# Mamba recurrence in pairs of tiles: 1024-column products and scans, states in SBUF over their inputs

## The chip, the core and the metric

The kernel runs on one core of a Trainium2 chip, as one launch. The metric is the device time of that launch in microseconds, lower being better. The core's engines work side by side and meet at semaphores: PE (TensorE, matrix products into PSUM), DVE (VectorE, elementwise work and scans), ACT (ScalarE, activation functions), POOL (GpSimd, elementwise work and indirect transfers) and SP (SyncE, which here issues most transfers). SBUF is the working memory of 128 partitions, PSUM the smaller memory that PE writes. All values here are fp32.

## The reference, cut to what matters

The program is a two-layer hybrid network over 32 sequences of 256 tokens and 128 features. The change concerns its first block alone, a bidirectional Mamba: 256 inner channels, 16 states per channel, forward and backward.

```python
def step(h, inp):
    u_t, d_t, B_t, C_t = inp
    dA = jnp.exp(d_t[..., None] * A)
    h = dA * h + (d_t * u_t)[..., None] * B_t[:, None, :]
    y = jnp.sum(h * C_t[:, None, :], axis=-1)
    return (h, y)
h0 = jnp.zeros((Bb, D_INNER, D_STATE), x.dtype)
_, ys = lax.scan(step, h0, xs)
y = jnp.transpose(ys, (1, 0, 2)) + xc * Dskip
y = y * jax.nn.silu(z)
return y @ out_w.T
...
y_f = _mamba(xn, ...)
y_b = jnp.flip(_mamba(jnp.flip(xn, 1), ...), 1)
y = jnp.concatenate([y_f, y_b], axis=-1) @ proj_w.T + proj_b
return x + y
```

After it come expert blocks, a tanh recurrence and two attention blocks with routed experts. They are the same before and after the change.

## The kernel before

The residual stays in SBUF as 16 tiles `xs[c]` of 128 features x 512 tokens (two sequences). The Mamba stage runs 32 units, `unit(k)`: chunk `k // 2`, forward for even k and backward for odd k. A unit is a Python generator; `pipeline(unit, 16, 2 * NCH)` starts a new one every 16 yields, so that the preparation of one unit (norm, convolution, projections, softplus) is traced beside the recurrence of the one before. The framework orders the instructions of each engine from this trace when it schedules them, by readiness and priority; so the order on an engine can differ from the order in the code. `behind_scans()` holds a DVE instruction behind the last scan traced.

**Preparation.** L425 to L530 make the activated input `act`, the step sizes `delta`, `du = delta * act` and the `gate`. Softplus is done with ACT functions and then three DVE instructions over 128x1024 values, L508 to L510, all of whose tensors lie in SBUF; the product L511 is POOL's. `delta` and `du` go to DRAM and come back (L545) as `widedelta` and `widedu`, with 4 states' copies on neighbouring partitions; B and C come back as `bcB` and `bcC` (L534). All these transfers are issued on SP.

**Recurrence.** A unit has two halves h of the channels, and in each four groups g of four tiles k. A tile is 128 partitions (32 channels x 4 states) x 512 columns. For each tile:

- L602, ACT: `dA = exp(A * delta)` into one of three PSUM banks `dAs`, taken in turn. Columns 0 and 256 stay zero from the memset at L407, so that the scan starts anew at each sequence.
- L606, POOL: `dBu = du * B`, 128x512, in SBUF.
- L615, DVE: the scan `h = dA * h + dBu`. Tiles 0 to 2 write their states to PSUM (`h2`), tile 3 to SBUF (`hs`). The backward direction reads and writes in reverse.
- The product with C: one DVE instruction for tiles 0 and 1 together (L617, 128x1024), one for tile 2 (L625, 128x512); tile 3 goes to POOL (L563)[...]. Of L617's and L625's operands, the states lie in PSUM and `bcC` in SBUF.

The weighted states of a group are summed over the 4 states of each channel by PE into the bank `yps` (L568), together with the skip product (L566). `summed` for one group is called after the second tile of the next. After four groups, DVE multiplies `yps` by the gate (L584); the backward unit also projects and adds to the residual (L637, L638).

[...]: three `dAs`, two `m`, two `hs`, one `yps`.

Of the kernel before, what the change touches and what calls it, by code (L numbers as in the profile page):

```python
# [13 lines left out]
F32 = mybir.dt.float32  # L14
# [3 lines left out]
AF = mybir.ActivationFunctionType  # L18
ALU = mybir.AluOpType
# [3 lines left out]
P = 128  # L23
B, L = 32, 256
NT = B * L
CH = 512
# [247 lines left out]
def hybrid_kernel(ctx: ExitStack, tc, x_d, out_d, d, packs):  # L274
    nc = tc.nc
# [14 lines left out]
    def K(name):  # L290
        return cst.view(cst_t, name) if name in cst.at else cst1.view(late_t["cst1"], name)
# [10 lines left out]
    def two(ap):  # L302
        return ap.rearrange("p (b t) -> p b t", b=2)
# [48 lines left out]
    with ExitStack() as ph:  # L352
# [7 lines left out]
        wconv, wout, A, skip = {}, {}, {}, {}  # L360
        with tc.tile_pool(name="mtap", bufs=1) as tp, tc.tile_pool(name="mprep", bufs=2, space=PSUM) as pp:
            tap_t = tp.tile([P, tap.n], F32, name="tap_t")
            nc.scalar.dma_start(tap_t, d["tap"].partition_broadcast(P))
            for k, s in enumerate("fb"):

                wconv[s] = wp.tile([P, DCONV, DI], F32, name="wconv" + s)
                at, _, w = tap.at[s]
# [20 lines left out]
        p2 = ph.enter_context(tc.tile_pool(name="m2", bufs=2))  # L388
        ps = ph.enter_context(tc.tile_pool(name="mps", bufs=2, space=PSUM))
# [7 lines left out]
        outs, turn, scan = {}, [0], [None]  # L397

        def behind_scans():

            return tc.issue_after(scan[0].ins) if scan[0] else nullcontext()

        dAs = [ps.tile([P, CH], F32, name=f"dA{k}", bufs=1) for k in range(3)]
        for t in dAs:
            nc.vector.memset(two(t)[:, :, 0:1], 0.0)  # L407

        def rows_of(ap, at, dims, n_rows):

            return bass.AP(ap.tensor, ap.offset + at * CH, [[a * CH, n] for a, n in dims] + [[1, n_rows * CH]])

        def unit(k):
            c, s = k // 2, "fb"[k % 2]
# [5 lines left out]
            def both(tag, bufs):  # L420
                return p2.tile([P, 2, CH], F32, tag=tag, name=tag, bufs=bufs)
# [45 lines left out]
            for h in range(2):  # L467
                for j in range(DCONV):
                    at = j if s == "f" else 2 * PAD - j
# [4 lines left out]
                        start=(j == 0),  # L474
                        stop=False,
# [5 lines left out]
            act = both("act", 2)  # L481
# [38 lines left out]
            for h in range(2):  # L520
# [4 lines left out]
                    start=True,  # L525
                    stop=True,
                )
            yield
            gate = both("gate", 2)
            nc.scalar.activation(gate, m, AF.Silu)  # L530
            bc = {}
# [9 lines left out]
            def load(h):  # L541
                out = []
                for n in ("delta", "du"):
                    t = p2.tile([P, 4, CH], F32, tag="wide" + n, name="wide" + n)
                    nc.sync.dma_start(  # L545
                        t.rearrange("p k t -> p (k t)"), rows_of(wide_d[n], h * P, ((4, 32), (0, 4)), 4)
                    )
                    out.append(t)
                return out
# [5 lines left out]


            sums, ended = None, None
            yps = None

            def summed(h, g, prods, hs):  # L560
                nonlocal yps, ended
                pr = p2.tile([P, CH], F32, tag="prod", name="pr", bufs=4)
                nc.gpsimd.tensor_mul(pr, hs, bc["C"][:, g, :])  # L563
                if g == 0:
                    yps = ps.tile([P, CH], F32, tag="y", name="yps", bufs=1)
                    nc.tensor.matmul(yps, skip[s][:, h, :], act[:, h, :], start=True, stop=False, skip_group_check=True)  # L566
                for k, pr in enumerate([*prods, pr]):
                    nc.tensor.matmul(  # L568
                        yps[32 * k : 32 * k + 32, :],
                        K("states"),  # L570
                        pr,
                        start=False,
                        stop=(g == 3),
                        skip_group_check=True,
                        tile_position=(0, 32 * k),
                    )
                if g == 3:
                    ended = h

            def gated():  # L580
                nonlocal ended
                yg = p2.tile([P, CH], F32, tag=f"yg{s}{ended}", name="yg", bufs=1)
                with behind_scans():
                    nc.vector.tensor_mul(yg, yps, gate[:, ended, :])  # L584
                outs[s, ended] = yg
                ended = None

            for h in range(2):
                dw, duw = wide[h]
                for g in range(4):  # L590
                    if (h, g) == (0, 1):
                        wide.append(load(1))

                    h2 = ps.tile([P, 2, CH], F32, tag="hs", name="h2", bufs=1)
                    pr2 = p2.tile([P, 2, CH], F32, tag="prod2", name="pr2", bufs=2)
                    prods = [pr2[:, 0, :], pr2[:, 1, :]]
                    for k in range(4):
                        dA = dAs[turn[0] % 3]
                        turn[0] += 1
                        at = 16 * h + 4 * g + k  # L600
                        steps = dw[:, k, :] if s == "f" else dw[:, k, ::-1]
                        nc.scalar.activation(  # L602
                            two(dA)[:, :, 1:L], two(steps)[:, :, 1:L], AF.Exp, scale=A[s][:, at : at + 1]
                        )
                        dBu = p2.tile([P, CH], F32, tag="dBu", name="dBu", bufs=4)
                        nc.gpsimd.tensor_mul(dBu, duw[:, k, :], bc["B"][:, g, :])  # L606
                        if k == 3:
                            hs = p2.tile([P, CH], F32, tag="hs", name="hs")
                        elif k == 2:
                            h2 = ps.tile([P, 2, CH], F32, tag="hs", name="h2", bufs=1)  # L610
                            hs = h2[:, 0, :]
                        else:
                            hs = h2[:, k, :]
                        views = (hs, dA, dBu) if s == "f" else (hs[:, ::-1], dA, dBu[:, ::-1])
                        scan[0] = nc.vector.tensor_tensor_scan(*views, 0.0, ALU.mult, ALU.add)  # L615
                        if k == 1:
                            nc.vector.tensor_mul(pr2, h2, bc["C"][:, g, :].unsqueeze(1).to_broadcast([P, 2, CH]))  # L617
                            yield
                            if ended is not None:
                                gated()  # L620
                            if sums:
                                summed(*sums)
                        elif k == 2:
                            pr = p2.tile([P, CH], F32, tag="prod", name="pr", bufs=4)
                            nc.vector.tensor_mul(pr, hs, bc["C"][:, g, :])  # L625
                            prods.append(pr)
                    sums = (h, g, prods, hs)
                    yield
            yield
            summed(*sums)  # L630
            yield
            gated()
            yield
            if s == "b":
# [4 lines left out]
                yield  # L639

        pipeline(unit, 16, 2 * NCH)

    late = ctx.enter_context(tc.tile_pool(name="late", bufs=1))
# [1066 lines left out]
```

## Time and profile before

| | us |
|---|---|
| median of 3 runs | 6272.99 |
| the three runs | 6271.46 to 6285.75 |
| profiled execution, its own time | 6280.36 |
| profiled execution, its span | 6278.6 |

| engine, whole span | busy us | share |
|---|---|---|
| PE | 5317.6 | 85% |
| DVE | 4184.9 | 67% |
| POOL | 3335.2 | 53% |
| ACT | 2664.6 | 42% |

The shares are means over stages with different limits. The Mamba stage takes about the first third: between 60 and 2100 us DVE is busy for 1866.63 us, POOL for 1770.79, PE for 1447.34 and ACT for 1170.29. Lines of the profile name the source line, the engine, the operation, the tile written and those read, shapes and count, and then busy time and mean duration in ns of one instruction, followed by the engine's idle time ahead of them and what ended it. A line of the timeline gives the start and the duration in us.

### The profile page before, as it was taken

To read this page: it belongs to the slowest core of one execution; us is meant where nothing else is said; L and a number is where in the kernel's file an instruction comes from. 1 tells how busy PE (TensorE), PEld (TensorE's weight loads), DVE (VectorE), ACT (ScalarE), POOL (GpSimd) and SP (SyncE) were. 2 spreads that over 40 slices of the span, in tenths; PEclk is the share of its full clock that TensorE was granted. 3 is DMA by queue.
4 is the path that set the end of the run, shared out by engine and by line. 5 is a ranking of instruction groups with operands and counts; after the bars stand their busy time and mean duration, and the time that the engine had idled before them with its cause. 6 is when DMAs were issued, how large, how long until landed. Compare 5 with 4: busy or idle time off the path is not lost. (4 is left out here: it accounts for less than half of the span.)

```text
span 6278.6 us, 73286 instructions
## 1 busy us (share of the span) xinstructions
PE 5317.6 (85%) x25538; PEld 2731.4 (44%) x25538; DVE 4184.9 (67%) x7070; ACT 2664.6 (42%) x4376; POOL 3335.2 (53%) x3074
## 2 busy tenths in 40 slices
PE   6777777777776799999989889897998999998897
PEld 2111111111111366865534444445884444444786
DVE  5999999999999664044645555554665666664565
ACT  4565555556565355334524434432221333333221
POOL 5888888888888565034634444443332333333332
PEclk8887888888888899588989999998998999997998
DMA  3232233322332660000000000003550000000555
GB/s 153 115 122 115 108 129 121 116 108 112 119 122 114 235 257 1 1 1 1 1 1 8 9 10 8 8 11 104 188 188 22 18 18 18 18 11 11 188 187 187
DMA packets 190417, 512.08 MB, mean 82 GB/s; under 512 B 22176, under 2 KB 75168, under 8 KB 164960
## 3 DMA queue, kind: packets, MB, share of 16 engines
q1 hardware_dynamic: 172192, 468.00, 20.7%
q0 software_dynamic: 17280, 35.69, 1.7%
q8 instruction: 202, 3.31, 0.2%
q10 hardware_dynamic: 576, 3.71, 0.2%
q14 instruction: 167, 1.37, 0.1%
HBM read 359.93 MB, written 147.38 MB: 81 GB/s over the span
## 5 line engine op out<-in xcount | busy, mean ns | idle before, releaser
L606 POOL TENSOR_TENSOR dBu<-widedu,bcB 128x512 f32<-128x512 f32 x1024 | 1334.0, 1324 | 250.7 <-DVE h L615 132.8
L615 DVE TENSOR_TENSOR_SCAN h<-dA,dBu 128x512 f32<-128x512 f32 x768 | 941.3, 1226 | 108.7 <-ACT dA L602 37.8
L568 PE MATMUL yps<-pr,cst_t 128*32 128x512 f32 x2048 | 702.5, 719 | 300.0 <-POOL pr L563 129.4
L930 POOL TENSOR_SCALAR_AFFINE_SELECT e<-e 128x2048 f32<-128x2048 f32 (+1 forms) x256 | 343.1, 1352 | 600.7 <-ACT e L1041 388.5
L1406 POOL DMA_INDIRECT rows_out<-y,goes x284 | 271.8, 957 | 558.5 <-DVE y L1404 451.5
L602 ACT ACTIVATE dA<-widedelta,Af 128x510 f32<-128x510 f32 x512 | 351.3, 689 | 398.4 <-DVE h L615 311.0
L994 DVE TENSOR_REDUCE nm<-st 128x2 f32<-128x512 f32 x512 | 324.3, 684 | 267.6 <-PE st L990 266.7
L602 ACT ACTIVATE dA<-widedelta,Ab 128x510 f32<-128x510 f32 x512 | 346.9, 687 | 354.5 <-DVE h L615 237.1
L568 PEld LDWEIGHTS yps<-pr,cst_t 128*32 128x32 f32 x2048 | 98.8, 120 | 870.2 <-POOL pr L563 308.1
L1181 ACT ACTIVATE s<-s 128x512 f32<-128x512 f32 x284 | 179.0, 630 | 575.9 <-DVE s L1180 329.2
L314 POOL TENSOR_TENSOR rstd<-var,cst_t 128x4 f32<-128x4 f32 x128 | 130.0, 1016 | 514.0 <-DVE var L312 512.1
L775 POOL TENSOR_TENSOR comb<-comb,ye 128x512 f32<-128x512 f32 x224 | 284.7, 1275 | 181.2 <-DVE ye L774 74.8
L1054 ACT ACTIVATE e<-st 128x512 f32<-128x512 f32 x512 | 271.6, 599 | 178.0 <-PE st L1050 146.0
L563 POOL TENSOR_TENSOR pr<-hs,bcC 128x512 f32<-128x512 f32 x256 | 339.8, 1328 | 13.3 <-DVE hs L615 13.0
L615 DVE TENSOR_TENSOR_SCAN hs<-dA,dBu 128x512 f32<-128x512 f32 x256 | 308.9, 1207 | 16.5 <-ACT dA L602 16.5
L1295 POOL DMA_INDIRECT rows_in<-xt,slot x256 | 254.0, 992 | 119.5 <-issue 99.1
L617 DVE TENSOR_TENSOR pr<-h,bcC 128x1024 f32<-128x1024 f32 x256 | 309.9, 1210 | 7.8
L1182 DVE TENSOR_TENSOR hh<-s,u_ps 128x512 f32<-128x512 f32 x284 | 195.3, 688 | 169.8 <-ACT s L1181 165.5
L1387 PE MATMUL g_ps<-xb,gu 128*128 128x256 f32 x1136 | 302.1, 389 | 3.6 <-ACT xb L1370 2.3
L1396 PE MATMUL yps<-dn,hh 128*128 128x128 f32 x2272 | 290.6, 276 | 5.3 <-DVE hh L1182 5.3
L1387 PE MATMUL u_ps<-xb,gu 128*128 128x256 f32 x1136 | 293.4, 381 | 0.0
L1396 PEld LDWEIGHTS yps<-dn,hh 128*128 128x128 f32 x2272 | 282.4, 192 | 14.0 <-DVE hh L1182 6.8
(348 smaller groups left out, 11021.0 us busy)
## 6 DMA issues: line engine op xcount, KB each, us to landing
gu<-in_gu SPq DMA_DIRECT2D x142, 512.0 KB, 3.7
rows_in<-zero SPq DMA_DIRECT2D x60, 1170.0 KB, 18.7
widedelta<-delta_d SPq DMA_DIRECT2D x64, 1024.0 KB, 6.8
widedu<-du_d SPq DMA_DIRECT2D x64, 1024.0 KB, 5.1
dn<-in_dn SPq DMA_DIRECT2D x142, 256.0 KB, 3.9
bcB<-xdbl_d SPq DMA_DIRECT2D x32, 1024.0 KB, 5.3
bcC<-xdbl_d SPq DMA_DIRECT2D x32, 1024.0 KB, 7.2
xr<-rows_in SPq DMA_DIRECT2D x142, 130.0 KB, 3.9
```

Source lines behind the costliest of these rows:

```text
L563: nc.gpsimd.tensor_mul(pr, hs, bc["C"][:, g, :])
L568: nc.tensor.matmul(yps[32 * k : 32 * k + 32, :], K("states"), pr, start=False, stop=(g == 3), skip_group_check=True, tile_position=(0, 32 ...
L602: nc.scalar.activation(two(dA)[:, :, 1:L], two(steps)[:, :, 1:L], AF.Exp, scale=A[s][:, at : at + 1])
L606: nc.gpsimd.tensor_mul(dBu, duw[:, k, :], bc["B"][:, g, :])
L615: scan[0] = nc.vector.tensor_tensor_scan(*views, 0.0, ALU.mult, ALU.add)
L617: nc.vector.tensor_mul(pr2, h2, bc["C"][:, g, :].unsqueeze(1).to_broadcast([P, 2, CH]))
L775: nc.gpsimd.tensor_add(comb, comb, ye)
L930: nc.gpsimd.affine_select(e, e, [[0, n], [sign, P]], ALU.is_gt, 0.0, base=base, channel_multiplier=-sign)
L994: nc.vector.tensor_reduce(n1[:, x, 2 * r : 2 * r + 2], o.rearrange("p (j k) -> p j k", j=2), AX.X, ALU.max, negate=True,)
L1387: nc.tensor.matmul(o[:, j, :], gu[:, at : at + P], xb, start=True, stop=True)
L1396: nc.tensor.matmul(yps[:, t, :], hh[:, k, t * P : (t + 1) * P], dn[:, k, :], start=(k == 0), stop=(k == FF // P - 1),)
L1406: i = nc.gpsimd.indirect_dma_start(rows_out[:, :], bass.IndirectOffsetOnAxis(ap=goes[:, t : t + 1], axis=0), y[:, t, :], None)
```

## The change

The four tiles of a group are handled as two pairs of 128x1024.

- `dAs` become two tiles of two PSUM banks each, taken in turn by pairs. ACT still writes 128x512 at a time; backward, the two halves are swapped, and ACT reads the steps in reverse.
- One POOL product over 1024 columns writes `du * B` of a pair into an SBUF tile `hs` (six buffers). One DVE scan over 1024 columns runs in place, its states replacing their inputs. The zeros in `dA` separate the tiles of a pair as they do the sequences.
- The product with C is in place, too, over 1024 columns (`weigh`): on DVE for the first pair; for the second pair on POOL, except in the fourth group of a half, where it is DVE's. It is called for the second pair in `summed`, after the first pair of the next group.
- `yps` has two banks, one for each half; the states' two PSUM banks are gone.

The matmuls, the transfers and all other stages are unchanged.

```diff
-        dAs = [ps.tile([P, CH], F32, name=f"dA{k}", bufs=1) for k in range(3)]
+        dAs = [ps.tile([P, 2, CH], F32, name=f"dA{k}", bufs=1) for k in range(2)]
         for t in dAs:
-            nc.vector.memset(two(t)[:, :, 0:1], 0.0)
+            nc.vector.memset(t.rearrange("p k (b t) -> p (k b) t", b=2)[:, :, 0:1], 0.0)
...
-            def summed(h, g, prods, hs):
-                nonlocal yps, ended
-                pr = p2.tile([P, CH], F32, tag="prod", name="pr", bufs=4)
-                nc.gpsimd.tensor_mul(pr, hs, bc["C"][:, g, :])
+            yps = {}
+
+            def weigh(engine, hs, g):
+                engine.tensor_mul(hs, hs, bc["C"][:, g, :].unsqueeze(1).to_broadcast([P, 2, CH]))
+
+            def summed(h, g, pairs):
+                nonlocal ended
+                weigh(nc.vector if g == 3 else nc.gpsimd, pairs[1], g)
                 if g == 0:
-                    yps = ps.tile([P, CH], F32, tag="y", name="yps", bufs=1)
-                    nc.tensor.matmul(yps, skip[s][:, h, :], act[:, h, :], start=True, stop=False, skip_group_check=True)
-                for k, pr in enumerate([*prods, pr]):
+                    yps[h] = ps.tile([P, CH], F32, tag="y", name="yps")
                     nc.tensor.matmul(
-                        yps[32 * k : 32 * k + 32, :],
+                        yps[h], skip[s][:, h, :], act[:, h, :], start=True, stop=False, skip_group_check=True
+                    )
+                for k in range(4):
+                    nc.tensor.matmul(
+                        yps[h][32 * k : 32 * k + 32, :],
                         K("states"),
-                        pr,
+                        pairs[k // 2][:, k % 2, :],
...
-                    nc.vector.tensor_mul(yg, yps, gate[:, ended, :])
+                    nc.vector.tensor_mul(yg, yps[ended], gate[:, ended, :])
...
-                    h2 = ps.tile([P, 2, CH], F32, tag="hs", name="h2", bufs=1)
-                    pr2 = p2.tile([P, 2, CH], F32, tag="prod2", name="pr2", bufs=2)
-                    prods = [pr2[:, 0, :], pr2[:, 1, :]]
-                    for k in range(4):
-                        dA = dAs[turn[0] % 3]
+                    pairs = []
+                    for half in range(2):
+                        dA = dAs[turn[0] % 2]
                         turn[0] += 1
-                        at = 16 * h + 4 * g + k
-                        steps = dw[:, k, :] if s == "f" else dw[:, k, ::-1]
-                        nc.scalar.activation(
-                            two(dA)[:, :, 1:L], two(steps)[:, :, 1:L], AF.Exp, scale=A[s][:, at : at + 1]
+                        for k in range(2):
+                            at = 16 * h + 4 * g + 2 * half + k
+                            steps = dw[:, 2 * half + k, :]
+
+                            a = dA[:, k if s == "f" else 1 - k, :]
+                            steps = steps if s == "f" else steps[:, ::-1]
+                            nc.scalar.activation(
+                                two(a)[:, :, 1:L], two(steps)[:, :, 1:L], AF.Exp, scale=A[s][:, at : at + 1]
+                            )
+
+                        hs = p2.tile([P, 2, CH], F32, tag="hs", name="hs", bufs=6)
+                        nc.gpsimd.tensor_mul(
+                            hs, duw[:, 2 * half : 2 * half + 2, :], bc["B"][:, g, :].unsqueeze(1).to_broadcast([P, 2, CH])
                         )
-                        dBu = p2.tile([P, CH], F32, tag="dBu", name="dBu", bufs=4)
-                        nc.gpsimd.tensor_mul(dBu, duw[:, k, :], bc["B"][:, g, :])
-                        if k == 3:
-                            hs = p2.tile([P, CH], F32, tag="hs", name="hs")
-                        elif k == 2:
-                            h2 = ps.tile([P, 2, CH], F32, tag="hs", name="h2", bufs=1)
-                            hs = h2[:, 0, :]
-                        else:
-                            hs = h2[:, k, :]
-                        views = (hs, dA, dBu) if s == "f" else (hs[:, ::-1], dA, dBu[:, ::-1])
-                        scan[0] = nc.vector.tensor_tensor_scan(*views, 0.0, ALU.mult, ALU.add)
-                        if k == 1:
-                            nc.vector.tensor_mul(pr2, h2, bc["C"][:, g, :].unsqueeze(1).to_broadcast([P, 2, CH]))
+                        flat = hs.rearrange("p k t -> p (k t)")
+                        flat = flat if s == "f" else flat[:, ::-1]
+                        scan[0] = nc.vector.tensor_tensor_scan(
+                            flat, dA.rearrange("p k t -> p (k t)"), flat, 0.0, ALU.mult, ALU.add
+                        )
+                        pairs.append(hs)
+                        if half == 0:
+                            weigh(nc.vector, hs, g)
                             yield
...
-                        elif k == 2:
-                            pr = p2.tile([P, CH], F32, tag="prod", name="pr", bufs=4)
-                            nc.vector.tensor_mul(pr, hs, bc["C"][:, g, :])
-                            prods.append(pr)
-                    sums = (h, g, prods, hs)
+                    sums = (h, g, pairs)
```

More of the change, by code (lines that the diff above doesn't have):

```diff
@@ L557, in unit @@
             sums, ended = None, None
-            yps = None
-            def summed(h, g, prods, hs):
-                nonlocal yps, ended
-                pr = p2.tile([P, CH], F32, tag="prod", name="pr", bufs=4)
-                nc.gpsimd.tensor_mul(pr, hs, bc["C"][:, g, :])
+            yps = {}
[4 more added lines that the diff above has]
+                weigh(nc.vector if g == 3 else nc.gpsimd, pairs[1], g)
                 if g == 0:
-                    yps = ps.tile([P, CH], F32, tag="y", name="yps", bufs=1)
-                    nc.tensor.matmul(yps, skip[s][:, h, :], act[:, h, :], start=True, stop=False, skip_group_check=True)
-                for k, pr in enumerate([*prods, pr]):
+                    yps[h] = ps.tile([P, CH], F32, tag="y", name="yps")
                     nc.tensor.matmul(
-                        yps[32 * k : 32 * k + 32, :],
+                        yps[h], skip[s][:, h, :], act[:, h, :], start=True, stop=False, skip_group_check=True
[3 more added lines that the diff above has]
+                        yps[h][32 * k : 32 * k + 32, :],
                         K("states"),
-                        pr,
+                        pairs[k // 2][:, k % 2, :],
                         start=False,
```

## The prediction

> **What bounds the kernel now.** I read the page's table of 40 slices first, because the change touches one stage only. The rows give the busy tenths of an engine in each 157 us slice.
>
> ```profile
> span 6278.6 us, 73286 instructions
> DVE  5999999999999664044645555554665666664565
> POOL 5888888888888565034634444443332333333332
> ```
>
> DVE  5999999999999664044645555554665666664565
>
> ```profile
> 300.00:1900.00 1600.00, 1141.22 (x2833) 295.80 (x2836) 1472.03 (x1400) 932.38 (x1183) 1398.17 (x1060) 0.83 0.31 118
> ```
> ```profile
> L606 POOL TENSOR_TENSOR dBu<-widedu,bcB 128x512 f32<-128x512 f32 x808 | 1053.7, 1325 | 192.5 <-DVE h L615 101.4 <-DVE hs L615 77.8 <-DVE var L440 9.4
> L615 DVE TENSOR_TENSOR_SCAN h<-dA,dBu 128x512 f32<-128x512 f32 x606 | 742.6, 1225 | 76.0 <-ACT dA L602 30.0 <-DVE h L615 0.5 <-DVE pr L625 0.5
> L563 POOL TENSOR_TENSOR pr<-hs,bcC 128x512 f32<-128x512 f32 x202 | 268.5, 1329 | 9.4 <-DVE hs L615 9.4
> L617 DVE TENSOR_TENSOR pr<-h,bcC 128x1024 f32<-128x1024 f32 x202 | 244.6, 1211 | 6.5
> L615 DVE TENSOR_TENSOR_SCAN hs<-dA,dBu 128x512 f32<-128x512 f32 x202 | 243.8, 1207 | 14.4 <-ACT dA L602 14.4
> L511 POOL TENSOR_TENSOR du<-delta,act 128x1024 f32<-128x1024 f32 x25 | 58.7, 2349 | 0.0
> L510 DVE TENSOR_TENSOR delta<-lg,du 128x1024 f32<-128x1024 f32 x25 | 30.1, 1204 | 0.0
> ```
>
> L508 starts first at 342.7 and for the 25th time at 1868.7 us: 24 units in 1526 us, **63.6 us per unit** (half-chunk and direction; 32 in all, in 8 groups of four scans each). Per unit, by the busy times, DVE works 58.5, POOL 55.6, ACT 37, PE 45. DVE sets the pace: in the last unit, where little else runs, one group follows the other every 6.94 us (scans at 2054.69 and 2061.63) with no gap that another engine explains. Eight of them are 55.5; the softplus, gate and norm instructions of a unit add about 6.2, and waits for ACT's dA 44.4/1600 x 63.6 = 1.8. That closes at 63.5. POOL has 8 us of slack.
>
> The view that decides is the stage's timeline around one softplus, where DVE reads two SBUF tensors (L508, L509, L510) while POOL multiplies (start, duration):
>
> ```profile
> 1104.02 3.47 POOL L606 TENSOR_TENSOR dBu<-widedu,bcB 128x512 f32<-128x512 f32 x2 [2.80 <-DVE hs L615]
> 1104.97 1.39 DVE L508 SCALAR_TENSOR_TENSOR sp<-sp,delta 128x1024 f32<-128x1024 f32 x1
> ...
> 1106.89 1.68 DVE L509 TENSOR_TENSOR lg<-lg,sp 128x1024 f32<-128x1024 f32 x1
> ...
> 1107.45 2.24 POOL L563 TENSOR_TENSOR pr<-hs,bcC 128x512 f32<-128x512 f32 x1
> ...
> 1109.62 1.20 DVE L510 TENSOR_TENSOR delta<-lg,du 128x1024 f32<-128x1024 f32 x1
> ...
> 1109.79 2.15 POOL L606 TENSOR_TENSOR dBu<-widedu,bcB 128x512 f32<-128x512 f32 x1
> ```
>
> POOL's product, otherwise 1.27 (two: 2.50), takes 3.47, 2.24 and 2.15: it lost 0.97, 0.97 and 0.88, on average **0.94 us for each such DVE instruction**. L509 asked at 1106.89 while POOL held on until 1107.45, and took 1.68 instead of 1.20. The two exclude each other. L617 does not show this today: its states lie in PSUM, and bcC is its only SBUF operand.
>
> **The change part by part.** Per unit, POOL first.
>
> dBu products: 32 of 128x512 (start to start 4.95/4 = 1.24 in a run of four) become 16 of 128x1024. Nearest row: L511, same engine and size, next POOL instruction 2.31 after it. C products on POOL (L563): 8 of 1.24 become 6 of 2.31. So POOL goes from 40 x 1.24 = 49.6 to 22 x 2.31 = 50.8, and everything else it does stays at 55.6 - 49.6 = 6.0. Fewer starts save little, since two products more of half-size moved to it.
>
> C products on DVE: 8 of L617 (1.21) and 8 of L625 (0.69) become 10 of 128x1024, and **both inputs are now in SBUF**. Nearest row: L510, 1.20; start to start 1.13 (L510 at 1109.62, next scan 1110.75). By itself DVE is relieved[...]. [...] The row says 0.94 lost by POOL per product, so 10 x 0.94 = 9.4[...]. POOL then needs 6.0 + 50.8 + 9.4 = **66.2 us per unit without a single idle moment, against a period of 63.6 today**. The lower end would be no loss (56.8), but three softplus instructions, unit after unit, show the loss with the same operand kinds. In the other direction DVE waits behind POOL: nothing at L510, 0.48 at L509, and behind a 2.31 product up to that.
>
> Scans: 32 of 1.225 become 16 of 1024 columns. No such scan is in the trace. Upper end 2 x 1.225 = 2.45 (nothing saved); lower end 1.225 + 0.53 = 1.76 (the second 512 columns at the rate of the products: L617 1.211 less L625 0.688). Two products of half the size cost 0.165 more than one, which puts the fixed part at 0.165, so I take 2.45 - 0.165 = 2.29, start to start 2.19. DVE per group: two scans 4.4, one product 1.2; with the two extra products and 6.2 of other work 8 x 5.7 + 2.3 + 6.2 = 54 per unit, down from 61.7. That DVE reads states from SBUF instead of PSUM is worth 1.211 - 1.204 = 7 ns a product by L617 and L510, or 0.1 us per unit[...].
>
> Exponentials: the same 32 ACT instructions of 0.69; four banks in pairs instead of three, so up to 1.8 us of waiting per unit may go, hidden under POOL's time. If POOL did not bind it would count in full. PE: the same five matmuls per group (skip only in the first); a second yps bank removes a wait of PE for L584, and PE waits on others already, so zero. Memsets: two instead of three, once. DMAs: none added or moved, so SP's queue is unchanged; POOL's queue gains no new kind of work.
>
> **One group, by hand.** Let S1(n) be the second scan of group n, ending at T. POOL's C product W1 runs to T + 0.08 + 2.31 = T + 2.39 (0.08: from the scan at 1025.31 to L606 at 1025.39). DVE's next scan S0 ends at T + 2.2, and its product W0 waits until 2.39 and holds POOL for 0.94. The dBu of the second pair then ends at T + 5.6, and S1(n+1) at T + 8.0, 0.1 for the signal. POOL fills S1's time with the next group's dBu. Queued behind the waiting W0 on DVE is that very scan, so the wait is not free. Six such groups: 48.0. In the other two, where the fourth group's product goes to DVE, two DVE products stand in line: if they run one after the other the group takes 6.8, if POOL takes the path between them 9.0; I take 7.9 each, 15.8. POOL's other work adds 6.0, since it delays POOL everywhere. Sum **69.8 us per unit**, 67.6 to 72.0 by the two ends; the floor is 66.2. Change: 6.2 x 32 = 198 us. From the profiled run's 6280.36 (span 6278.6) that is 6478; that run lies 7.4 over the median of 6272.99, so I forecast a median of **6471**.
>
> **Rivals.**
> - *Mutual waiting costs more* (0.16): the trace issues instructions in another order than the code (the k = 3 scan comes after the next group's first two), so the order is not mine to know. If DVE meets a POOL product of 2.31 at a random point it waits 1.15, 13 times a unit: 15 on DVE's 54, or 69, beside POOL's 66; two engines that are both full and wait for each other lose more, some 73 to 80 per unit, so 6574 to 6798. Against it: six hs buffers let POOL run ahead.
> - *The products get past each other* (0.09): should POOL's loss be small because DVE's products fall into POOL's waits for scans, DVE's 54 and POOL's 56.8 count, and with 2 of idle time 59: 4.6 x 32 = 147 less, 6126. It turns at a loss of (63.6 - 56.8)/10 = 0.68 us per product with POOL never idle. For it: POOL idles 8 us a unit today. Against: the loss was 0.88 or more in each of the three, and the product that follows its own scan at once finds POOL busy.
> - *The change does little* (0.03): losses just there, 6254 to 6292. More banks alone would also look so.
>
> **How the numbers follow.** My case has 0.72, with its own range 66.2 to 73 per unit, 6356 to 6574. A range of 6360 to 6620 leaves out the second and third rivals (0.12) and the upper part of the first (0.08). About 0.3% (19 us) can be told from no change: faster 0.09, same 0.03, slower 0.88.
>
> **What would show it.** Right: POOL above 93% in the stage, its 128x1024 products averaging 2.6 us or more instead of 2.35, with DVE's share falling to 85% or less, 128x1024 scans near 2.29, and L508 every 69 to 70 us. The prediction is wrong if POOL's products stay at 2.35 beside DVE's, or if POOL idles for scans (first rival), or if DVE's products show 2 us and more.

## The result and the profile after

| | before | after |
|---|---|---|
| median, us | 6272.23 | 6588.72 |
| runs, us | 6270.25 to 6285.75 | 6581.61 to 6597.97 |
| span of the profiled execution, us | 6278.6 | 6596.2 |
| first scan to the end of the last, us | 74.7 to 2098.3 | 76.5 to 2408.9 |
| from there to the end of the span, us | 4180.3 | 4187.3 |

The ratio is 1.0498, with an interval of 1.0483 to 1.0513: slower by 316 us. Of the 318 us between the profiled spans, 309 lie inside the Mamba stage; the rest of the program takes what it took. (DVE's row of the slices stands twice at the head of the prediction; it is one row, and its slices 2 to 13, with DVE at nine tenths or more, are the Mamba stage. The lines of windows there and below give, after the stretch and its length, the busy time and the instructions of PE, PEld, DVE, ACT and POOL in this order, then PE's granted clock.)

L508 starts for the first time in this window at 334.9 and for the 22nd time at 1857.7 us: 72.5 us per unit, after 63.6. The page's slices answer to the two rows shown of before:

```profile
DVE  5888898888888876503455655554565666665565
POOL 5888888888888866503462444444332233233232
```

The stage now fills 14.6 slices of 165 us, after 13.4 of 157, and DVE is no longer at nine tenths all through, while POOL has not risen. The window from 300 to 1900 us and the groups by shape in it:

```profile
300.00:1900.00 1600.00, 926.49 (x2465) 253.22 (x2464) 1417.36 (x731) 807.00 (x1026) 1396.98 (x525) 0.76 0.27 101
```
```profile
L612 POOL TENSOR_TENSOR hs<-widedu,bcB 128x1024 f32<-128x1024 f32 x350 | 921.5, 2655 | 189.4 <-PE yps L572 187.0 <-DVE hs L561 2.4
L617 DVE TENSOR_TENSOR_SCAN hs<-dA,hs 128x1024 f32<-128x1024 f32 x349 | 786.0, 2274 | 26.0 <-POOL hs L612 14.0 <-ACT dA L607 11.5
L561 DVE TENSOR_TENSOR hs<-hs,bcC 128x1024 f32<-128x1024 f32 x217 | 480.0, 2227 | 2.2
L561 POOL TENSOR_TENSOR hs<-hs,bcC 128x1024 f32<-128x1024 f32 x131 | 371.0, 2835 | 0.0
```

DVE's product of 128x1024 with C took 1.21 us with its states in PSUM (L617 of before) and takes 2.23 with its states in SBUF, from 1.19 to 3.38 over the stage: the waiting is inside the instruction, so it counts as busy. POOL's products take 2.66 and 2.84, where 2.35 was the time of such a product (L511) before. And POOL stands idle 189.4/1600 x 72.5 = 8.6 us per unit, nearly all of it until PE's sums (L572) let an `hs` buffer go. Per unit DVE is busy for 64.2 us and POOL for 63.3, of 72.5. A stretch of the timeline shows both kinds of loss:

```profile
2195.13 2.34 POOL L612 TENSOR_TENSOR hs<-widedu,bcB 128x1024 f32<-128x1024 f32 x1 [0.73 <-PE yps L572]
...
2196.56 1.99 DVE L561 TENSOR_TENSOR hs<-hs,bcC 128x1024 f32<-128x1024 f32 x1
...
2197.44 3.32 POOL L561 TENSOR_TENSOR hs<-hs,bcC 128x1024 f32<-128x1024 f32 x1
...
2200.81 1.94 PE L572 MATMUL yps<-hs,cst_t 128*32 128x512 f32 x8 [5.77 <-POOL hs L561]
...
2202.86 4.48 DVE L561 TENSOR_TENSOR hs<-hs,bcC 128x1024 f32<-128x1024 f32 x2
2202.89 3.37 POOL L612 TENSOR_TENSOR hs<-widedu,bcB 128x1024 f32<-128x1024 f32 x1 [2.13 <-PE yps L572]
```

DVE's product is issued at 2196.56 while POOL's runs until 2197.47; it takes 1.99 instead of 1.2 and ends 1.08 after POOL's, so it did its work once POOL was done. POOL's next product, issued at 2197.44, takes 3.32, about 1.0 more. Only when that one ends, at 2200.76, may PE sum and release buffers; POOL, whose next instruction is a dBu without a buffer, idles for 2.13. Then the two meet again: two DVE products take 4.48 instead of 2.4, the dBu 3.37.

A third loss lies ahead of the softplus. L508 before and after, and one such wait:

```profile
L508 DVE SCALAR_TENSOR_TENSOR sp<-sp,delta 128x1024 f32<-128x1024 f32 x25 | 35.1, 1405 | 18.4 <-ACT lg L506 18.4
```
```profile
L508 DVE SCALAR_TENSOR_TENSOR sp<-sp,delta 128x1024 f32<-128x1024 f32 x22 | 33.1, 1506 | 116.2 <-ACT lg L506 116.2
```
```profile
1043.54 13.55 POOL L612 TENSOR_TENSOR hs<-widedu,bcB 128x1024 f32<-128x1024 f32 x5
...
1057.05 3.35 POOL L561 TENSOR_TENSOR hs<-hs,bcC 128x1024 f32<-128x1024 f32 x1
...
1060.45 1.93 PE L572 MATMUL yps<-hs,cst_t 128*32 128x512 f32 x8 [9.96 <-POOL hs L561]
...
1062.32 2.99 PE L521 MATMUL m<-xpad,mam_t 128*128 128x512 f32 x4
...
1065.34 1.02 ACT L530 ACTIVATE gate<-m 128x1024 f32<-128x1024 f32 x1 [7.58 <-PE m L521]
...
1067.68 1.06 ACT L506 ACTIVATE lg<-sp 128x1024 f32<-128x1024 f32 x1
...
1068.77 1.79 DVE L508 SCALAR_TENSOR_TENSOR sp<-sp,delta 128x1024 f32<-128x1024 f32 x1 [10.56 <-ACT lg L506]
```

POOL's C product stands behind five dBu. PE's sums wait for it, and PE's projection for the gate (L521) comes after them; ACT's `gate` waits for that, ACT's `lg` (L506) comes after `gate`, and DVE idles for 10.56 us. This happens in every second unit: 5.3 us per unit on average, after 0.7. In the kernel before, ACT never waits for `gate`'s input in this window; now it does in each unit, for 170.9 us in all.

### The profile page after: what moved, and what is told of

Its sections match the earlier page's. It is cut to its first block, busy times and chain, and to the rows that moved or that the text cites. A ratio compares the mean times of both kernels' runs of the same rounds, so it can differ in the third digit from the quotient of the medians.

```text
span 6596.2 us, 71693 instructions
## 1 busy us (share of the span) xinstructions
PE 5205.8 (79%) x25466; PEld 2725.2 (41%) x25538; DVE 4401.3 (67%) x6365; ACT 2660.8 (40%) x4376; POOL 3610.9 (55%) x2498
## 5 line engine op out<-in xcount | busy, mean ns | idle before, releaser
L612 POOL TENSOR_TENSOR hs<-widedu,bcB 128x1024 f32<-128x1024 f32 x512 | 1351.3, 2662 | 279.0 <-PE yps L572 267.6
L617 DVE TENSOR_TENSOR_SCAN hs<-dA,hs 128x1024 f32<-128x1024 f32 x512 | 1152.7, 2274 | 58.8 <-POOL hs L612 35.0
L572 PE MATMUL yps<-hs,cst_t 128*32 128x512 f32 x2048 | 544.8, 811 | 818.7 <-POOL hs L561 741.3
L561 DVE TENSOR_TENSOR hs<-hs,bcC 128x1024 f32<-128x1024 f32 x320 | 711.5, 2238 | 3.4
L572 PEld LDWEIGHTS yps<-hs,cst_t 128*32 128x32 f32 x2048 | 73.2, 125 | 1197.5 <-POOL hs L561 906.6
L561 POOL TENSOR_TENSOR hs<-hs,bcC 128x1024 f32<-128x1024 f32 x192 | 547.5, 2854 | 3.9 <-DVE hs L617 3.9
L765 PE MATMUL m<-x,com_t 128*128 128x512 f32 x512 | 271.4, 612 | 0.0
```

Of the source, the lines that this page charges most:

```text
L561: engine.tensor_mul(hs, hs, bc["C"][:, g, :].unsqueeze(1).to_broadcast([P, 2, CH]))
L572: nc.tensor.matmul(yps[h][32 * k : 32 * k + 32, :], K("states"), pairs[k // 2][:, k % 2, :], start=False, stop=(g == 3), skip_group_check= ...
L612: nc.gpsimd.tensor_mul(hs, duw[:, 2 * half : 2 * half + 2, :], bc["B"][:, g, :].unsqueeze(1).to_broadcast([P, 2, CH]))
L617: scan[0] = nc.vector.tensor_tensor_scan(flat, dA.rearrange("p k t -> p (k t)"), flat, 0.0, ALU.mult, ALU.add)
```

## The experiments

A chain of waits that closes on itself is called a ring below. Three theories were set against each other, and a fourth after the first four runs. None of them had the wait for `lg` in it, and no run changed that alone. **A**: a DVE instruction with two SBUF inputs and a POOL product exclude each other, as the softplus of the kernel before had it (0.94 us of POOL's lost to each), and that is the loss. **B**: the six `hs` buffers, each held from dBu to PE's sum, bind. **C**: in-place work or states in SBUF are slow by themselves. **D**, the later one: the order in which POOL's two kinds of product stand makes POOL, DVE and PE wait in a ring.

All ratios are to the kernel before, run on the same chip; its median was 6311 in the first two batches and 6280 and 6275 in the last two, so ratios are compared and not times. Where an expectation is a time, I read it against the 6590 of the changed kernel.

**Ones in PSUM for DVE's products.** It leaves out the C weights of the tiles that DVE multiplies.

```diff
+        cC = ps.tile([P, CH], F32, name="cC", bufs=1)
+        nc.vector.memset(cC, 1.0)
...
-                engine.tensor_mul(hs, hs, bc["C"][:, g, :].unsqueeze(1).to_broadcast([P, 2, CH]))
+                by = cC if engine is nc.vector else bc["C"][:, g, :]
+                engine.tensor_mul(hs, hs, by.unsqueeze(1).to_broadcast([P, 2, CH]))
...
-                    yps[h] = ps.tile([P, CH], F32, tag="y", name="yps")
+                    yps[h] = ps.tile([P, CH], F32, tag="y", name="yps", bufs=1)
```

> Edit: the changed kernel with one yps bank; the freed bank holds ones, and DVE's products take it as second factor in place of bcC (the C weights of these tiles are left out). Same count, shape and place of instructions, but only one SBUF input. Theory A (DVE and POOL exclude each other through the second SBUF input): DVE's product falls from 2.24 to about 1.2 us, POOL's dBu from 2.66 to 2.35, a unit from 72.5 to 57 to 63 us, the whole to 6100 to 6290. Theory B (the six hs buffers bind, POOL waits for PE to let one go): POOL's idle stays near 8.6 us a unit and the whole at 6350 or more. Theory C (in-place products or states in SBUF are slow by themselves): DVE's product stays near 2.2 us and the time near 6590.

Ratio 1.0201 (1.0180 to 1.0221). The groups of this run:

```profile
L616 POOL TENSOR_TENSOR hs<-widedu,bcB 128x1024 f32<-128x1024 f32 x379 | 906.7, 2416 | 242.5 <-PE yps L576 221.1 <-DVE hs L621 21.3
L565 DVE TENSOR_TENSOR hs<-hs,cC 128x1024 f32<-128x1024 f32 x236 | 282.8, 1215 | 3.6
```

The same in-place product takes 1.215 us, from 1.205 to 1.222 in all 236, as soon as its second factor lies in PSUM. So theory C falls and the exclusion is shown on both sides, for POOL's dBu falls, too, from 2.66 to 2.42. Its share of the loss is not the whole: a unit takes 67.0 us ((1851.1 - 309.8)/23), 5.5 of the 8.9 come back (4.7 against the control below), and now DVE (55.0 busy) idles for 12 us and POOL (56.2) for 11. DVE still waits 101.7 us of the window for `lg`, 4.3 per unit. A's size was wrong: POOL's wait for buffers (221.1) did not go, as B had it, and B's bound for the time was met. Both fit, and the rest had to be looked for in what keeps the buffers held.

**The control with one yps bank.** Only the last line of the diff above.

> Edit: the changed kernel with one yps bank instead of two, nothing else: the control for the runs that use that bank. A, B and C alike: 6560 to 6650. Over 6650 would say that the second bank is worth something in itself.

Ratio 1.0456 (1.0434 to 1.0477), 71.7 us per unit. The second bank gains nothing here, and the run above may be read against the changed kernel.

**Seven buffers.** `bufs=7` for `hs`.

> Edit: seven hs buffers instead of six. Theory B: POOL's idle of 8.6 us a unit falls to 5 or less, and the whole by 100 to 200, to 6390 to 6490. Theory A: POOL's lead turns into more waiting of DVE at its products; the whole stays within 50 of 6590.

Ratio 1.0480 (1.0449 to 1.0511): no change. POOL's wait for PE fell from 187.0 to 109.3 us of the window, but other waits took its place, and no time came of it, as A said:

```profile
L612 POOL TENSOR_TENSOR hs<-widedu,bcB 128x1024 f32<-128x1024 f32 x351 | 948.5, 2727 | 152.9 <-PE yps L572 109.3 <-issue 21.6 <-DVE xin L456 13.6
```

One buffer more is not what is missing, though this doesn't rule out that many more would do it.

**dBu in halves.**

```diff
-                        nc.gpsimd.tensor_mul(
-                            hs, duw[:, 2 * half : 2 * half + 2, :], bc["B"][:, g, :].unsqueeze(1).to_broadcast([P, 2, CH])
-                        )
+                        for k in range(2):
+                            nc.gpsimd.tensor_mul(hs[:, k, :], duw[:, 2 * half + k, :], bc["B"][:, g, :])
```

> Edit: the dBu product of a pair in two POOL instructions of 128x512 instead of one of 128x1024. POOL has 16 more starts a unit, some 0.17 us each, 2.7 us. Theory A, by way of DVE waiting for the whole POOL instruction: DVE's mean product falls from 2.24 to 1.7 or 1.8, and the whole to 6440 to 6560. If the length of POOL's instruction doesn't matter (B, C): 6600 to 6680.

Ratio 1.0492 (1.0468 to 1.0515). DVE's mean product fell to 1.92, less than expected, beside dBu instructions of 1.53 instead of 2.66; but it took 1.92 in the control, too, where dBu is whole (2.71), so the fall can't be put down to their length. POOL's busy time rose to 66.0 of 72.4 us. A miss of the expected gain: what DVE saved, POOL spent. (The expectation's 0.17 for a start is an estimate, 2 x 1.24 - 2.31 of the prediction.)

**All C products on DVE.**

```diff
-                weigh(nc.vector if g == 3 else nc.gpsimd, pairs[1], g)
+                weigh(nc.vector, pairs[1], g)
```

> Edit: all products with C go to DVE, in place and from SBUF; POOL keeps the 16 dBu products of a unit. POOL's own work falls to 6 + 16 x 2.31 = 43 us a unit, DVE's rises to 16 x 2.19 + 16 x 1.13 + 6.2 = 59. Theory A (each such product waits some 1.0 us for POOL): DVE 59 + 16 = 75 a unit, the ratio to the kernel before 1.05 to 1.07. If POOL's sum of work and losses is what binds (43 + 16 x 0.94 = 58): ratio 0.97 to 1.00. Theory D (the order in which POOL's C products and dBu products stand, with PE and the hs buffers waiting for the former, binds): no C product is left on POOL, so ratio under 1.02.

Ratio 1.0432 (1.0396 to 1.0469). In the window DVE is never free, and POOL is idle a third of the time:

```profile
300.00:1900.00 1600.00, 1005.99 (x2524) 258.81 (x2520) 1589.91 (x881) 827.63 (x1051) 1054.62 (x404) 0.73 0.27 104
```

1589.91 of 1600 with 71.1 us per unit: DVE's 59 of work plus waits, its product at 1.93 on average. A comes nearest, but its range of 1.05 to 1.07 is missed (it said 75 us; the wait was 0.7 and not 1.0). That POOL's sum alone or the order alone should bind falls here.

**C from PE.** PE spreads the C row of a group over the partitions, in place of DVE's reading of `bcC`, for the first pair of each group. (`yps` has one bank for it, and `xdbl` a third buffer.)

```diff
+                            cb = ps.tile([P, CH], F32, tag="cb", name="cb", bufs=1)
+                            nc.tensor.matmul(cb, M("selC")[:, g * P : (g + 1) * P], xdbl, start=True, stop=True)
-                            weigh(nc.vector, hs, g)
+                            weigh(nc.vector, hs, g, cb)
```

> Edit: one yps bank; in the freed bank PE spreads a group's C row over the partitions (one matmul of 0s and 1s with xdbl per group), and DVE's product of the first pair takes C from there, one SBUF input instead of two. Two products a unit (second pair of the fourth group) still read two. Theory A with what the run with ones showed (67.0 us a unit, ratio 1.020): eight of ten products freed, 67 to 68.5, ratio 1.020 to 1.035. If the added matmul gets in the way of the sums on PE: over 1.04.

Ratio 1.0366 (1.0335 to 1.0398), just above the range of A and under the 1.04 of the other: DVE waited 153.0 of the window's 1600 us for `cb`, while PE's sums, in the same queue, waited 270.9 for POOL.

**POOL in the traced order.**

```diff
+                        with (tc.issue_after(pooled[0].ins) if pooled[0] else nullcontext()):
                             nc.gpsimd.tensor_mul(hs, duw[...], ...)
```

`pooled[0]` is POOL's last C product.

> Edit: on POOL a dBu product may not stand ahead of a C product that was traced before it (issue order only); this gives the order by which one group was worked out by hand in the prediction. Theory D (the order costs some 3 us a unit, by which the hand count of 69.8 was short of 72.5): 69 to 70.5 a unit, ratio 1.030 to 1.040. Theory A alone (mutual exclusion, in any order): ratio 1.045 to 1.055.

Ratio 1.0458 (1.0427 to 1.0489), 71.7 us per unit. Theory D in this form falls. The waits only moved:

```profile
L620 DVE TENSOR_TENSOR_SCAN hs<-dA,hs 128x1024 f32<-128x1024 f32 x354 | 803.7, 2280 | 151.5 <-POOL hs L615 149.2
L561 POOL TENSOR_TENSOR hs<-hs,bcC 128x1024 f32<-128x1024 f32 x133 | 322.3, 2424 | 156.5 <-DVE hs L620 151.2
```

POOL's dBu products no longer wait for buffers; DVE's scans now wait for dBu, and POOL's C products for scans. This is the ring of the prediction's hand count (scan, C product, dBu, scan).

**Both: C from PE and the traced order.**

> Edit: both, C of the first pairs from PSUM and POOL's products in the traced order. A and D together: a group is then scan 2.29, C product 2.31, dBu 2.31 and 0.2 of signals, 7.1 us in six groups of a unit, some 6.8 in two, and part of POOL's other 6: 60 to 63 a unit, ratio 0.965 to 1.00. A alone: like the run without the pinned order, 1.020 to 1.035.

Ratio 1.0108 (1.0075 to 1.0141), 65.1 us per unit. Each edit alone brought 1.0366 and 1.0458, together they bring much more; yet the ring is still seen (scans wait 176.3 for dBu, POOL's C products 119.7 for scans), and the expected gain over the kernel before is missed.

**Later sums, with C from PE.** The sums of a group, with POOL's C product, are traced behind the second pair of the next group.

```diff
                         if half == 0:
                             weigh(nc.vector, hs, g, cb)
                             yield
+                        else:
                             if ended is not None:
                                 gated()
                             if sums:
                                 summed(*sums)
```

> Edit: C of the first pairs from PSUM, as before; and the sums of a group, with POOL's C product, are traced after the second pair of the next group instead of after the first, dBu products still not ahead of them. On POOL the C product then always stands behind two dBu products, so that its scan is long done, and the next scan needn't wait for it. Theory D (the run in the traced order, 65.1 us a unit, was held by the loop scan, C product, dBu, scan): the loop is gone, POOL's sum binds, 57 + 5 x 0.94 = 61.5 us a unit, 61 to 63, ratio 0.965 to 0.995. If the six hs buffers bind as soon as they are held longer (theory B): 65 or more, ratio over 1.01.

Ratio 1.0063 (1.0047 to 1.0078), 65.1 us per unit, like the run before and not as expected. Buffers are not the reason: POOL waited for them for 12.4 us of the window. A shorter ring stays around the fourth group, where DVE takes both products and POOL idles for 3.4 us.

**Later sums alone**, with C from SBUF in all products: the instructions of the changed kernel, in another order.

> Edit: the changed kernel with that later place of the sums and POOL's order kept, C still from SBUF in all products. Theory A (exclusion sets a floor whatever the order): POOL's sum with its losses is 66.2 us a unit, so no less than 66, ratio no lower than 1.02, and 1.03 to 1.05 if DVE's waits of 1.0 us per product go on. Theory D alone (order): like the run before it, under 1.00.

Ratio 1.0263 (1.0246 to 1.0280), 68.3 us per unit: above A's floor, far from D's "under 1.00", and a little below the 1.03 to 1.05 that A gave if DVE's waits went on, although they did. The window and DVE's product:

```profile
300.00:1900.00 1600.00, 1096.72 (x2618) 269.72 (x2616) 1558.32 (x776) 863.49 (x1098) 1528.33 (x557) 0.77 0.28 109
```
```profile
L561 DVE TENSOR_TENSOR hs<-hs,bcC 128x1024 f32<-128x1024 f32 x231 | 581.8, 2531 | 2.0
```

DVE is busy for 97% of the window and POOL for 96%. Neither idles for long; both are full because each waits inside its instructions for the other (DVE's product at 2.53, where it took 1.215 with one factor in PSUM; POOL's dBu at 2.87, where L511 of before took 2.35). DVE's wait for `lg` is 11.6 us of the window, 0.5 per unit after 5.3. POOL's busy time is 65.2 us per unit, next to the 66.2 that the prediction had as its floor; only C from PE, in the same order, goes below (the run before this one, 2% better).

**A pair on the kernel before.** Two tiles of a group as a pair, states in PSUM.

```diff
-                        dA = dAs[turn[0] % 3]
+                        dA = dA1 if k > 1 else dA2[:, k if s == "f" else 1 - k, :]
...
+                            nc.gpsimd.tensor_mul(dBu2, duw[:, 0:2, :], ...)
...
-                            hs = h2[:, k, :]
+                            hs, dA, dBu = (t.rearrange("p k t -> p (k t)") for t in (h2, dA2, dBu2))
```

> Edit: from the kernel before, only the first two tiles of a group as a pair: dA in two adjoining banks, one dBu product and one scan over 1024 columns, states still in PSUM; tiles 2 and 3 as before, with one dA bank between them (prod has two buffers instead of four to make room). No product has two SBUF inputs. Theory A: the pair alone saves 2 x 1.225 - 2.275 = 0.18 and a start, some 0.3 us a group, 2.4 a unit: ratio 0.985 to 1.00, up to 1.01 if the one dA bank makes DVE wait for ACT. If 1024-column scans or pairs as such were the harm: over 1.02.

Ratio 1.0062 (1.0049 to 1.0075), in the last part of the range. Groups with no wait stand 6.86 us apart (pair scans at 1006.14 and 1013.00 us), against 6.94 before; the pair saves no more. What the run lost elsewhere fits the two buffers of `prod`: DVE waited 50.0 us of the window for PE's sums ahead of L632, which writes there; its wait for ACT's dA hardly grew (48, after 44). Pairs as such do no harm of size here, and no good.

**All second products on POOL**, on the run with later sums and C from PE.

```diff
-                w = weigh(nc.vector if g == 3 else nc.gpsimd, pairs[1], g)
-                if g != 3:
-                    pooled[0] = w
+                pooled[0] = weigh(nc.gpsimd, pairs[1], g)
```

> Edit: from the run with C from PSUM and the later sums: the second pair's product of the fourth group goes to POOL as well, so that no product with C on DVE has two SBUF inputs and POOL's order is two dBu, one C product throughout. POOL: 24 x 2.31 + 6 = 61.4 us a unit, DVE some 52. Theory D with A: the waits of POOL at the fourth group (3.4 us, twice a unit) go, POOL is full, 61.5 to 63.5, ratio 0.97 to 1.00. If the hs buffers bind when they are held longer (B): 65 or more, ratio 1.00 to 1.02.

Ratio 1.0092 (1.0070 to 1.0113), 65.4 us per unit, 1508.11 of 1600 us busy on POOL: 61.6 per unit, as counted, and 3.8 idle, nearly all for scans. No version beat the kernel before. With POOL's own work at 57 to 61.6 us per unit, 63.6 leaves little room for any wait.

## Why the prediction was right, and where it was off

**Direction and cause: right.** The forecast rested on DVE's products becoming readers of two SBUF tensors. The run with ones in PSUM takes that alone away: the product falls from 2.23 to 1.215, and the ratio from 1.046 (the control) to 1.020, more than half of the loss. What would bind was not right: I had POOL full, and it idles.

**The range: in part by luck.** The median of 6589 lies in the range of 6360 to 6620, but above my case's own 6356 to 6574. The range holds it because it took in the lower part of the first rival.

**Scans: right.** 2.274 measured, 2.29 worked out.

**POOL's loss: nearly right.** Per unit, from the page's means, (2.662 - 2.349) x 16 + (2.854 - 2.349) x 6 = 8.0 us; I took 9.4. POOL's busy time of 63.3 is below the 66.2 of the sum, and the order with later sums brings it to 65.2 with the unit at 68.3. (POOL's C products grew by four of half size, not by two as I wrote; the 50.8 has it right.)

**The term that was mis-sized: 69.8 us for a unit, measured 72.5.** Over 32 units that is 198 us against 285; the rest of the 316 lies at the ends of the stage and behind it. Three entries of the hand count were too small.

- *DVE's wait at a product.* I let W0 wait 0.2 us in six groups of eight, since POOL's C product would end just then. On average it waits 2.24 - 1.21 = 1.03, at 10 products. I had put 1.15 per product into the first rival only, and its lower end, 73, is what came: that rival described the result better than my case.
- *POOL's idle time.* I counted POOL as never idle, with "six hs buffers let POOL run ahead" as the reason against that rival. It idles 8.6 us per unit for want of such a buffer: where POOL's C product comes late behind several dBu, PE's sums come late, and the buffers stay held.
- *The softplus.* I left it as it was, within 6.2 us of other work. Its three instructions read two SBUF tensors too, and now take 5.9 us per unit after 4.0; and DVE's wait for `lg`, for which I had no entry, grew by 4.5.

On DVE, then, C products make a unit 6.5 us longer (15.2 to 21.8), the softplus 1.9 and the wait for `lg` 4.5; the scans make it 3.6 shorter (39.2 to 35.6). These sum to 9.3, where the unit grew by 8.9.

With the later order the same instructions take 68.3, so 4.2 us of a unit were order. In it DVE's wait for `lg` falls by 4.8 while its products wait longer; how much of the 4.2 is that wait, and how much the buffers, no run separates. It was not the order I drew: pinning that one gave 71.7.

**Signs I named.** POOL's products above 2.6: yes. POOL over 93% of the stage: no, 87%. DVE at 85% or less: no, 89%, since the time that a DVE product waits for POOL is shown as busy. L508 every 69 to 70 us: no, 72.5. And one sign of being wrong came true: DVE's products at 2 us and more (2.23). POOL did idle, too, though for PE's sums and not for scans.

**Off the path, as said:** the second yps bank (the control, without it, is no slower). The four dA banks were not tried alone; DVE's wait for dA fell from 1.8 to 0.5 us per unit. PE's own work was no limit (busy for 58% of the window), but with L521 behind the sums it passed POOL's delay on to ACT and DVE. PE's granted clock in the window was lower than before, 0.76 after 0.83; whether that cost anything was not tried.

What stays open: why units with C from PE and a regular order still stop at 65 and not at the 61.5 of POOL's sum. Rings of waits between scans, dBu and C products are seen in each, but no run took them all away.

## What to carry to other kernels

Before states are moved from PSUM to SBUF, count the DVE instructions that will then read two SBUF tensors (such a product took 2.23 us here, after 1.21), and count the waiting on both engines: here DVE was 92% busy and POOL 87%, and they could not take it. An engine that is "busy" may be waiting inside an instruction, so compare the mean with that of the same form elsewhere. Then follow each engine's largest idle entry back through the queues, also where the change touched nothing: here a late POOL product held DVE up in the softplus, by way of PE and ACT. And count how long a buffer is held, not only how many there are: a seventh brought no time, another order of the same instructions 4.2 us per unit.

## What the runs showed of the hardware

- The exclusion costs both sides: in the changed kernel DVE lost 1.03 us per product and POOL 0.31 (dBu) to 0.50 (C product) on average, where in the softplus read in the kernel before three DVE instructions cost POOL 0.94 each on average, and L509 waited 0.48. What a product waits is not fixed by how busy POOL is: 0.71 us in the control (POOL busy for 88% of the window), 1.02 in the changed kernel (87%), 0.72 with all products on DVE (66%), 1.32 with the later sums alone (96%).
- A scan with one input in PSUM and one in SBUF isn't touched in the changed kernel: all 512 took 2.255 to 2.292 us beside a POOL that was busy for 87% of the window. Twice the columns took 2.274/1.225 = 1.86 times as long.
- Halving POOL's dBu (two of 1.53, 3.06 together, for one of 2.66) went with a product of DVE that took 0.3 us less (1.92 for 2.23), as it did in the control with dBu whole, and cost POOL 0.4.
